# Transposes of x, B and the squares' sums moved from TensorE to VectorE squares of 32 placed by DMA

## The chip, the cores and the metric

The kernel runs on one core of one Trainium2 chip. The core has TensorE (PE in the profile, its weight loads PEld), VectorE (DVE), ScalarE (ACT), GpSimd (POOL), SyncE (SP), which here only issues transfers, and 16 DMA engines. The metric is the device time of one launch in microseconds; lower is better. The profile adds one execution under the hardware profiler.

## What is computed

A transformer-like layer in float32 on x of shape (8, 2048, 256): a layer norm with modulation from a condition, a state-space (Mamba-2) mixer, a gated residual, a second modulated layer norm, and a mixture of 8 experts whose weights are thresholded. All eight experts are computed for every token. The mixer, cut to what the change touches:

```python
zxbcdt = hidden_states @ W_in                    # z | x, B, C | dt
xBC = silu(causal_dwconv(xBC, conv_w, conv_b))   # 4 taps along the tokens
dt = softplus(dt + dt_bias)
# per chunk: scores C B^T times the decays, applied to x*dt; the state
# carries sum over tokens of B (x*dt) decay
y = ssd(x, dt, A, B, C) + x * D
y = y * silu(z)
y = y * rsqrt(mean(y * y, axis=-1) + EPS) * norm_w
return y @ W_out
```

## The kernel before, in words

The tokens are worked in 32 blocks of T = 512 (8 batch rows times 4), each in 4 chunks of 128. Channels lie on the 128 partitions and tokens along the free dimension after the projection: `xbc` holds x in four tiles of 128 channels (MI = 4), then B, then C.

The order of the work is a plan in Python. Each stage is a generator; `at` and `after` give due times, `until` waits for a step of the same plan, and a heap pops the stages by time (lines 192 to 209). The unit is meant as a microsecond, but only the order of emission comes out of it: the engines' queues and the framework's waits do the rest. Blocks start every PERIOD = 70 units; `STARTS` (L803) sets when each stage of a block is due, so several blocks are in work at once. The PSUM banks are handed out by the plan too: eight, with at most 3 for experts, 2 for projections, 2 for y, and 4 for everything else.

The stages of a block in order: `fetch` loads x; `first_norm` normalises and transposes it (L353, L355). `project_xbc` (L424) multiplies by the weights; `conv` adds the first tap on ACT (L379) and the three others on VectorE (L387). `steps_of_time` computes the decays and writes them to DRAM as `cs_d` (L505). `silu_xbc` (L442) and `project_z` (L460, silu in L447) follow. `spread` (L523) reads back the decays of a chunk over all partitions as `wide`. `within` handles a chunk: eight Relu steps on ACT (L538), four transposes of x (L548) and one of B (L549) on TensorE into two banks, the scores B^T C (L551), two exponentials (L552, L553); then on VectorE `xdt` = x times dt (L556) and `both` = (B, masked scores) out of PSUM (L560), on POOL `xdec` (L568), on VectorE `w` (L572), on POOL `cw` = C times decay (L575). L586 is the state's matmul, L589 and L600 carry the state on. For every two chunks `outputs` computes y (L618), adds D*x on VectorE, four instructions per chunk (L630), multiplies by silu(z) (L634), and sums squares over groups of channels into `sqs` (ACT L641, POOL L643, L644). `output` turns `sqs` on TensorE (L659), reduces it over the channels (L662), takes the inverse root, and multiplies by W_out (L672). Then come `residual`, `gate_weights`, and `experts` (matmuls L791, weighted sums on VectorE L748, last steps on POOL L756, L758, the store L761).

All transfers but one are issued by SP in order. An issue whose buffer is not free holds up those behind it.

Of the kernel before, what the change touches and what calls it, by code (L numbers as in the profile page):

```python
# [15 lines left out]
P = 128  # L16
# [4 lines left out]
EPS = 1e-5  # L21
GATE_MIN = 0.25
# [3 lines left out]
def kernel(  # L26
# [209 lines left out]

    def per_head(t):
        return t.unsqueeze(2).to_broadcast([P, NH, HEADDIM])
# [57 lines left out]
    def batch_gates(b):  # L296

        rows = new(pb, [P, KD, P], "rows", bufs=1)
# [77 lines left out]
    def conv(n, m, ps):  # L376

        acc = info[n]["xbc"][:, m, :]
        nc.scalar.activation(  # L379
# [53 lines left out]
    def silu_xbc(n):  # L433
# [3 lines left out]
        if order[n][1] > 0:  # L437
            yield from until(d, "fixed")
            nc.vector.tensor_add(xbc[:, :, :HALO], xbc[:, :, :HALO], info[n]["fix"])
            yield 0.4  # L440
        for m in range(0, MC, 2):
            nc.scalar.activation(xbc[:, m : m + 2, :], xbc[:, m : m + 2, :], AF.Silu)  # L442
            yield 2.0
        d["xbc_silu"] = True

# [73 lines left out]
    def spread(n, c):  # L519

        yield from until(info[n], "cs_d")
        wide = info[n]["wide", c] = new(chk, [P, NH, P], "wide")
# [3 lines left out]
        yield  # L526

    def within(n, c):
# [8 lines left out]
        for h in range(NH):  # L537
            nc.scalar.activation(  # L538
                w[:, h, :], wide[:, h, :], AF.Relu, bias=tok_major[:, 1, c, h : h + 1], scale=-1.0
            )  # L540
# [4 lines left out]
        yield from until(d, "xbc_silu")  # L545
        x_ps, b_ps = yield from take("m", 2)
        for m in range(MI):
            nc.tensor.transpose(x_ps[:, ts(m, P)], xbc[:, m, tok], ident)  # L548
        nc.tensor.transpose(b_ps[:, :P], bt, ident)  # L549

        nc.tensor.matmul(b_ps[:, P : 2 * P], bt, ct_, start=True, stop=True)  # L551
        nc.scalar.activation(wide, wide, AF.Exp)  # L552
        nc.scalar.activation(w, w, AF.Exp, scale=-1.0)  # L553
        yield 1.2
        xdt = new(chk, [P, DI], "xdt", bufs=3)
        nc.vector.tensor_tensor(  # L556
            by_head(xdt), by_head(x_ps[:, :DI]), per_head(tok_major[:, 0, c, :]), ALU.mult
        )
        both = new(chk, [P, 2, P], "both")
        nc.vector.tensor_mul(both, b_ps[:, : 2 * P].rearrange("p (n i) -> p n i", n=2), masks)  # L560
        bm, sm = both[:, 0, :], both[:, 1, :]
        give(x_ps)
        give(b_ps)
        last = s_of(n) == NSB - 1 and c == NC - 1
        yield 1.0
        if not last:
            xdec = new(chk, [P, DI], "xdec", bufs=1)
# [5 lines left out]
        yield 1.8  # L573
        cw = new(chk, [P, NH, P], "cw", bufs=3)
        nc.gpsimd.tensor_tensor(cw, wide, ct_[:, None, :].to_broadcast([P, NH, P]), ALU.mult)  # L575
        yield 2.0
# [4 lines left out]
        yield 3.5  # L581
        state = carry.get("state") if (s_of(n), c) != (0, 0) else None
        if not last:
# [3 lines left out]
            behind = new(blk, [P, DI], "state", bufs=4)  # L587
            if state is not None:
                nc.gpsimd.tensor_tensor(  # L589
                    by_head(behind), by_head(state), per_head(wide[:, :, P - 1]), ALU.mult  # L590
# [15 lines left out]
    def outputs(n, first):  # L606
# [17 lines left out]
        for j, y_ps in enumerate(pair):  # L624
# [4 lines left out]
            for m in range(MI):  # L629
                nc.vector.scalar_tensor_tensor(  # L630
                    y[:, m, :], xbc[:, m, tok], d_ch[:, m : m + 1], y[:, m, :],
                    ALU.mult, ALU.add,
                )
# [7 lines left out]
            nc.scalar.activation(sq, g[:, :, tok], AF.Square)  # L641
# [9 lines left out]
    def output(n):  # L651
# [4 lines left out]
        yield 5.0  # L656
        s_ps = yield from take("m")
        for c in range(NC):
            nc.tensor.transpose(s_ps[:, ts(c, P)], d["sqs"][:, c, :], ident)  # L659
        yield 1.2  # L660
        ms = new(sml, [P, NC], "ms")
        nc.vector.tensor_reduce(ms, s_ps.rearrange("p (c t) -> p c t", c=NC), AX.X, ALU.add)  # L662
        give(s_ps)
# [80 lines left out]
    def weighted(n, c, e, ps, res):  # L744
        wt = info[n]["wt"]
        per = 512 // DM
        for q in range(per):
            nc.vector.scalar_tensor_tensor(  # L748
# [16 lines left out]
    def experts(n):  # L765
# [34 lines left out]
    READ_TIME = 4.5  # L800
    WARM = 15
    PERIOD, XBC_STEP, Z_STEP, OUT_STEP = 70.0, 6.0, 3.5, 4.4
    STARTS = (  # L803
        (fetch, -20.0), (first_norm, -9.0), (project_xbc, 11.5), (project_z, 42.0),
        (silu_xbc, 47.5), (output, 128.0), (gate_weights, 156.0), (experts, 198.0),
# [6 lines left out]
    at(30.0, modulation(1))  # L812
    for n in range(len(order)):
        start = n * PERIOD
        for stage, delay in STARTS:
# [40 lines left out]
```

## Time and profile before

The profiled execution's numbers, with the median beside them:

| | |
|---|---|
| median of 3 runs | 2382.57 us (2381.75 to 2382.87) |
| the profiled execution's own time | 2381.93 us |
| its span, first to last instruction | 2380.1 us |
| mean granted TensorE clock | 0.993 of full speed |
| costliest group: expert matmuls, L791 | 2048 instructions, 963.3 us busy |
| costliest group of VectorE: weighted sums, L748 | 1024, 487.5 us busy |
| costliest group of ACT: Relu steps, L538 | 1024, 328.0 us busy |
| costliest group of POOL: `cw`, L575 | 128, 310.8 us busy |
| DMA packets | 64648 with 110.50 MB, 7096 of them under 512 B |

How to read the lines that follow: a group line names line, engine, operation, output <- inputs, their shapes (partitions x elements) and the count; after the first bar the busy time of the group and the mean length of one instruction in ns; after the second the idle time of its engine just before it and what ended that. The timeline gives start and length of each run of equal instructions. A line of stretches gives the stretch, its length, the busy us of the engines with the number of instructions, the granted clock, the mean busy share of the 16 DMA engines and GB/s. In the slices a digit is a tenth.

### The profile page before, as it was taken

The numbers are of one execution on the slowest core, as the hardware profiler recorded it, in microseconds if no ns is written. First come the engines' busy times: TensorE is split into PE (matmuls) and PEld (weight loads), VectorE is DVE, ScalarE is ACT, GpSimd is POOL, SyncE is SP. The second block draws the span as 40 slices with busy tenths as digits, with TensorE's granted clock in tenths as the row PEclk, the third lists the DMA queues.
The fourth block names the chain that finished last, engine by engine and source line by source line (L and its number), as shares of the span: only waits on it lengthen the run. The fifth ranks groups of instructions, "written<-read, shape, count | busy, mean of one in ns | idle before, by whom it ended". The sixth has DMA issues, their size and how long they took to land.

```text
span 2380.1 us, 33341 instructions
## 1 busy us (share of the span) xinstructions
PE 2317.9 (97%) x11632; PEld 1313.3 (55%) x11632; DVE 1816.6 (76%) x4188; ACT 1621.7 (68%) x2950; POOL 1128.4 (47%) x1245
## 2 busy tenths in 40 slices
PE   7899999999999999999999999999999999999998
PEld 4555555555555555555555555555555555555564
DVE  4777877778777787877877777878777787777775
ACT  6878766677666686666776667766776767667720
POOL 3554355453454454454544554544545444545442
PEclk8999999999999999999999999999999999999999
DMA  5111111110111111111110111111111101111100
GB/s 166 46 37 46 37 46 46 45 55 27 47 55 47 45 46 38 46 52 49 45 46 28 55 55 36 55 37 37 55 44 47 46 29 54 46 45 46 38 19 18
DMA packets 64648, 110.50 MB, mean 46 GB/s; under 512 B 7096, under 2 KB 47072, under 8 KB 64480
## 3 DMA queue, kind: packets, MB, share of 16 engines
q1 hardware_dynamic: 64464, 108.35, 13.8%
q8 instruction: 93, 1.52, 0.3%
q14 instruction: 75, 0.61, 0.1%
q10 hardware_dynamic: 16, 0.01, 0.0%
HBM read 89.47 MB, written 18.87 MB: 46 GB/s over the span
## 4 chain that ended last, share of the span: by engine, by line
PE 61%; ACT 10%; POOL 9%; DVE 6%; issue 1%; POOLq 0%; ACTq 0%; DVEq 0%
PE bank L791 26%; PE bank L672 8%; PE bank L424 7%; PE bank L460 6%; PE bank L618 4%; POOL cw L575 3%; PE bank L586 3%; ACT w L538 3%; DVE xbc L387 2%; PE bank L353 1%; PE bank L548 1%; ACT xbc L442 1%; POOL xdec L568 1%; POOL sq L643 1%; ACT wide L552 1%
## 5 line engine op out<-in xcount | busy, mean ns | idle before, releaser
L791 PE MATMUL bank<-we_sb,ht 128*128 128x512 f32 x2048 | 963.3, 595 | 3.3 <-DVE both L560 1.9
L748 DVE SCALAR_TENSOR_TENSOR res<-bank,wt,res 128x256 f32<-128x256 f32 x1024 | 487.5, 476 | 199.4 <-PE bank L791 112.7
L791 PEld LDWEIGHTS bank<-we_sb,ht 128*128 128x128 f32 x2048 | 374.0, 190 | 379.6 <-issue 352.1
L387 DVE SCALAR_TENSOR_TENSOR xbc<-bank,conv_w_sb,xbc 128x511 f32<-128x511 f32 (+2 forms) x576 | 425.8, 740 | 121.2 <-ACT halo L383 119.6
L575 POOL TENSOR_TENSOR cw<-wide,xbc 128x1024 f32<-128x1024 f32 x128 | 310.8, 2428 | 295.3 <-ACT wide L552 168.8
L538 ACT ACTIVATE w<-wide,tok_major 128x128 f32<-128x128 f32 x1024 | 328.0, 390 | 142.1 <-PE bank L618 100.8
L424 PE MATMUL bank<-ht,w_in_sb 128*128 128x512 f32 x768 | 369.1, 603 | 0.8 <-DVE xbc L387 0.8
L460 PE MATMUL bank<-ht,w_in_sb 128*128 128x512 f32 x512 | 244.4, 601 | 0.0
L672 PE MATMUL bank<-wo,zs 128*128 128x256 f32 x1024 | 243.5, 380 | 0.0
L589 POOL TENSOR_TENSOR state<-state,wide 128x512 f32<-128x512 f32 x112 | 120.8, 1079 | 232.7 <-DVE state L600 206.5
L424 PEld LDWEIGHTS bank<-ht,w_in_sb 128*128 128x128 f32 x768 | 140.4, 191 | 154.6 <-issue 139.5
L355 ACT ACTIVATE ht<-bank,mod_pp 128x512 f32<-128x512 f32 x128 | 97.4, 776 | 178.8 <-PE bank L353 178.7
L379 ACT ACTIVATE xbc<-bank,conv_b_sb,conv_w_sb 128x512 f32<-128x512 f32 x192 | 147.3, 767 | 104.3 <-PE bank L424 104.3
L672 PEld LDWEIGHTS bank<-wo,zs 128*128 128x128 f32 x1024 | 189.6, 191 | 48.9 <-issue 23.4
L568 POOL TENSOR_TENSOR xdec<-xdt,tok_major 128x512 f32<-128x512 f32 x120 | 142.0, 1183 | 141.9 <-DVE xdt L556 141.4
L756 POOL TENSOR_TENSOR res<-res,gates 128x256 f32<-128x256 f32 x128 | 134.9, 1054 | 151.8 <-DVE res L748 144.4
L343 ACT ACTIVATE xn<-xt,shift,rstd 128x256 f32<-128x256 f32 x256 | 137.5, 591 | 82.0 <-DVE shift L339 74.9
L572 DVE TENSOR_TENSOR w<-w,both 128x1024 f32<-128x1024 f32 x128 | 191.6, 1497 | 1.4
L630 DVE SCALAR_TENSOR_TENSOR bank<-xbc,d_ch,bank 128x128 f32<-128x128 f32 x512 | 175.6, 350 | 20.2 <-PE bank L618 10.9
L586 PE MATMUL bank<-xdec,both 128*128 128x512 f32 x240 | 128.6, 618 | 17.6 <-POOL xdec L568 12.8
L460 PEld LDWEIGHTS bank<-ht,w_in_sb 128*128 128x128 f32 x512 | 91.2, 191 | 96.5 <-issue 91.2
L643 POOL TENSOR_TENSOR sq<-sq 128x256 f32<-128x256 f32 x128 | 98.0, 766 | 91.3 <-ACT sq L641 73.4
(130 smaller groups left out, 3333.2 us busy)
## 6 DMA issues: line engine op xcount, KB each, us to landing
wide<-cs_d SPq DMA_DIRECT2D x128, 512.0 KB
out_dram<-xt SPq DMA_DIRECT2D x32, 512.0 KB
xt<-_attn_hidden_states_dram SPq DMA_DIRECT2D x31, 512.0 KB
cs_d<-cs SPq DMA_DIRECT2D x32, 64.0 KB
we_sb<-in_L_ffn_expert_w_dram SPq DMA_DIRECT2D x8, 256.0 KB
ht<-in_L_wmod_dram SPq DMA_DIRECT2D x2, 512.0 KB
w_in_sb<-in_L_attn_W_in_dram SPq DMA_DIRECT2D x1, 776.0 KB
xt<-_attn_hidden_states_dram SPq DMA_DIRECT2D x4, 128.0 KB
```

The lines of the kernel that those rows point to most:

```text
L387: nc.vector.scalar_tensor_tensor(acc[:, ahead:], ps[:, : T - ahead], conv_w_sb[:, m, k : k + 1], acc[:, ahead:], ALU.mult, ALU.add,)
L424: nc.tensor.matmul(ps, w_in_sb[:, k, DI + m * P : DI + (m + 1) * P], ht[:, k, :], start=(k == 0), stop=(k == KD - 1),)
L460: nc.tensor.matmul(ps, w_in_sb[:, k, ts(m, P)], ht[:, k, :], start=(k == 0), stop=(k == KD - 1),)
L538: nc.scalar.activation(w[:, h, :], wide[:, h, :], AF.Relu, bias=tok_major[:, 1, c, h : h + 1], scale=-1.0)
L568: nc.gpsimd.tensor_tensor(by_head(xdec), by_head(xdt), per_head(tok_major[:, 2, c, :]), ALU.mult)
L572: nc.vector.tensor_tensor(w, w, sm[:, None, :].to_broadcast([P, NH, P]), ALU.mult)
L575: nc.gpsimd.tensor_tensor(cw, wide, ct_[:, None, :].to_broadcast([P, NH, P]), ALU.mult)
L586: nc.tensor.matmul(st_ps[:, :DI], bm, xdec, start=True, stop=True)
L630: nc.vector.scalar_tensor_tensor(y[:, m, :], xbc[:, m, tok], d_ch[:, m : m + 1], y[:, m, :], ALU.mult, ALU.add,)
L672: nc.tensor.matmul(o_ps[:, :DM], d["zs"][:, m, ts(c, P)], wo[:, m, :], start=(m == 0), stop=(m == MI - 1),)
L748: nc.vector.scalar_tensor_tensor(res, ps[:, ts(q, DM)], wt[:, c, e + q : e + q + 1], res, ALU.mult, ALU.add)
L791: nc.tensor.matmul(ps, ht[:, k, ts(c, P)], we_sb[:, k, e : e + per, :].rearrange("p e o -> p (e o)"), start=(k == 0), stop=(k == KD - 1),)
```

## The change

Three transposes leave TensorE. In all blocks but the first, each of the four x tiles and the B tile is transposed by VectorE in squares of 32x32 (one instruction for 128 channels x 512 tokens), and four writes per tile put the squares' rows (runs of 32 numbers) at their turned place in a DRAM buffer `turned` (512 tokens x 640 channels). One load per chunk brings back 128 tokens x 640 channels as `xtok`, and x*dt is formed in place in it. In all blocks but the last, the squares' sums are transposed and reduced by VectorE in the same way: partial sums per group of 32 channels go to DRAM and come back by four loads, and a small reduce adds them. The first block keeps the transposes of x and B on TensorE, the last one those of the sums.

ACT multiplies x by D in place after the transpose has read it, so that one addition on VectorE replaces four instructions per chunk; the first block keeps the four. `cw` is now formed in the buffer of `wide` (four buffers instead of two), after the last column of `wide` was saved as `whole`, and earlier in the chunk. `xdec` gets a second buffer, `state` goes from four buffers to three. `rows` shares the buffer of `sign`. The mask for B is gone, since B is no longer multiplied by ones. `follow` adds an ordering, without a wait, behind the last marked instruction of the same engine. Several due times move: the table of starts is in the diff.

```diff
+    def follow(engine, second):
+        if engine in pace:
+            tc.add_manual_dep(
+                second.ins, pace[engine].ins.name,
+                mybir.DependencyInfo(mybir.DependencyClass.NoSync, mybir.DependencyReason.DATA),
+                reason="in the order of emission",
+            )
...
+        if n > 0:
+            d["turned"] = new(dram, [T, (MB + 1) * P], "turned")
         for m in range(0, MC, 2):
             nc.scalar.activation(xbc[:, m : m + 2, :], xbc[:, m : m + 2, :], AF.Silu)
-            yield 2.0
+            for q in range(m, min(m + 2, MB + 1) if n > 0 else m):
+                after(3.0 + 2.0 * (q - m), turn_tile(n, q))
+            yield 4.0 if n > 0 else 2.0
         d["xbc_silu"] = True
+
+    def turn_tile(n, m):
+
+        d = info[n]
+        squares = new(blk, [P, T], "squares", bufs=3)
+        nc.vector.transpose(squares, d["xbc"][:, m, :])
+        yield 2.5
+        places = d["turned"].rearrange("(b i) r -> i b r", i=SQ)
+        for a in range(P // SQ):
+            nc.sync.dma_start(
+                out=places[:, :, m * P + a * SQ :][:, :, :SQ],
+                in_=squares[ts(a, SQ), :].rearrange("i (b j) -> i b j", j=SQ),
+            )
+        d["turned", m] = True
+        yield 3.0
+        if m < MI:
+
+            x = d["xbc"][:, m, :]
+            follow("act", nc.scalar.activation(x, x, AF.Copy, scale=d_ch[:, m : m + 1]))
...
-        wide = info[n]["wide", c] = new(chk, [P, NH, P], "wide")
+        wide = info[n]["wide", c] = new(chk, [P, NH, P], "wide", bufs=4)
...
+    def turn(n, c):
+
+        d = info[n]
+        if n == 0:
+            return
+        yield from until(d, *(("turned", m) for m in range(MB + 1)))
+        xt = new(chk, [P, DI + P], "xtok", bufs=3)
+        nc.sync.dma_start(out=xt, in_=d["turned"][ts(c, P)])
+        yield TURN_TIME
+        d["xtok", c] = xt
...
-        yield from until(d, "xbc_silu")
-        x_ps, b_ps = yield from take("m", 2)
-        for m in range(MI):
-            nc.tensor.transpose(x_ps[:, ts(m, P)], xbc[:, m, tok], ident)
-        nc.tensor.transpose(b_ps[:, :P], bt, ident)
-
-        nc.tensor.matmul(b_ps[:, P : 2 * P], bt, ct_, start=True, stop=True)
         nc.scalar.activation(wide, wide, AF.Exp)
         nc.scalar.activation(w, w, AF.Exp, scale=-1.0)
+        yield from until(d, "xbc_silu")
+        yield 1.5
+
+        whole, cw = new(chk, [P, NH], "whole", bufs=3), wide
+        nc.gpsimd.tensor_copy(whole, wide[:, :, P - 1])
+        nc.gpsimd.tensor_tensor(cw, wide, ct_[:, None, :].to_broadcast([P, NH, P]), ALU.mult)
+        yield 1.5
+        yield from until(d, "xbc_silu" if n == 0 else ("xtok", c))
...
+        else:
+            s_ps = yield from take("m")
+
+        nc.tensor.matmul(s_ps[:, :P], bt, ct_, start=True, stop=True)
         yield 1.2
-        xdt = new(chk, [P, DI], "xdt", bufs=3)
-        nc.vector.tensor_tensor(
-            by_head(xdt), by_head(x_ps[:, :DI]), per_head(tok_major[:, 0, c, :]), ALU.mult
-        )
+        xdt, bm = d["xtok", c][:, :DI], d["xtok", c][:, DI:]
+        second = nc.vector.tensor_tensor(
+            by_head(xdt), by_head(x_ps[:, :DI] if n == 0 else xdt), per_head(tok_major[:, 0, c, :]),
+            ALU.mult,
+        )
...
-            xdec = new(chk, [P, DI], "xdec", bufs=1)
+            xdec = new(chk, [P, DI], "xdec")
...
+            if n > 0:
+                nc.vector.tensor_tensor(y, y, xbc[:, :MI, tok], ALU.add)
...
+            squares = new(blk, [P, T], "squares", bufs=3)
+            follow("dve", nc.vector.transpose(squares, d["sqs"].rearrange("p c t -> p (c t)")))
+            part = new(sml, [P, NC * NS], "part")
+            nc.vector.tensor_reduce(
+                part, squares.rearrange("p (q j) -> p q j", j=SQ), AX.X, ALU.add
+            )
+            yield 2.5
+            part_d = new(dram, [NS, SQ, NC, NS], "part_d")
+            nc.sync.dma_start(out=part_d.rearrange("a i c b -> (a i) (c b)"), in_=part)
+            yield 3.5
+            parts = new(sml, [P, NC, NS], "parts")
...
+                for q in range(NS):
+                    nc.sync.dma_start(
+                        out=parts[ts(q, SQ)].unsqueeze(3),
+                        in_=part_d[:, :, :, q : q + 1].rearrange("a i c b -> i c a b"),
+                    )
+            yield TURN_TIME
+            follow("dve", nc.vector.tensor_reduce(ms, parts, AX.X, ALU.add))
...
+    TURN_TIME = 12.0
...
-        (fetch, -20.0), (first_norm, -9.0), (project_xbc, 11.5), (project_z, 42.0),
-        (silu_xbc, 47.5), (output, 128.0), (gate_weights, 156.0), (experts, 198.0),
+        (fetch, -20.0), (first_norm, -9.0), (project_xbc, 11.5), (project_z, 48.0),
+        (silu_xbc, 47.5), (output, 144.0), (gate_weights, 190.0), (experts, 232.0),
...
+    first = {
+        project_z: 42.0, silu_xbc: 40.0, output: 112.0, gate_weights: 134.0, experts: 170.0,
+    }
...
-            at(start + c * PERIOD / NC + 44.0, spread(n, c))
-            at(start + c * PERIOD / NC + 54.0, within(n, c))
+            step = start + c * PERIOD / NC
+            at(step + (36.0 if n == 0 else 44.0), spread(n, c))
+            at(step + 59.0, turn(n, c))
+            at(step + (44.0 if n == 0 else 65.0), within(n, c))
```

## The prediction

> **What bounds the kernel now.** I read the page's busy lines first, then the wait list and the groups of TensorE by shape, then the timeline of one block, and last the transfers in narrow stretches. From the page, the busy time by engine and the slices:
>
> ```profile
> PE 2317.9 (97%) x11632; PEld 1313.3 (55%) x11632; DVE 1816.6 (76%) x4188; ACT 1621.7 (68%) x2950; POOL 1128.4 (47%) x1245
> PE   7899999999999999999999999999999999999998
> DMA  5111111110111111111110111111111101111100
> ```
>
> TensorE is in use almost everywhere, the next engine for 76%. A sum over three stretches (us from the start: length, then the busy us of PE, PEld, DVE, ACT, POOL, the granted clock, the DMA share, GB/s) shows where it is idle:
>
> ```profile
> 0.00:148.00 148.00, 119.50 (x646) 70.00 (x647) 102.31 (x224) 116.61 (x213) 65.54 (x87) 0.93 0.30 93
> 148.00:2310.00 2162.00, 2135.22 (x10796) 1212.03 (x10795) 1677.37 (x3876) 1499.58 (x2727) 1048.27 (x1139) 1.00 0.13 44
> 2310.00:2380.00 70.00, 63.22 (x193) 31.26 (x191) 36.89 (x89) 5.46 (x11) 14.57 (x21) 0.98 0.07 23
> ```
>
> Until the first expert matmul (148 us) 28.5 us are idle, in the last 70 us 6.8, and in the 2162 us between only 26.8. Each block takes about 72 us there (an output store at 1241.7, the next at 1314.1) and TensorE's work sets that. What it waits for most, by the wait list of PE (total us, times, longest), is small:
>
> ```profile
> PE bank L586 <- POOL xdec L568: 12.8, 22, 1.5
> PE bank L659 <- POOL sqs L644: 6.0, 4, 3.4
> ```
>
> So work taken from TensorE in the middle stretch shortens the kernel by as much, as long as nothing new makes TensorE wait.
>
> **What is taken from TensorE.** The three groups that go (busy us, mean ns, idle before), and one chunk of them in the timeline (start, us, instruction):
>
> ```profile
> L548 PE MATMUL bank<-ident,xbc 128*128 128x128 f32 x512 | 77.9, 274 | 2.7 <-ACT xbc L442 2.7
> L549 PE MATMUL bank<-ident,xbc 128*128 128x128 f32 x128 | 35.4, 277 | 3.7 <-ACT xbc L442 2.9 <-DVE xdt L556 0.8
> L659 PE MATMUL bank<-ident,sqs 128*128 128x128 f32 x128 | 20.4, 276 | 6.0 <-POOL sqs L644 6.0
> ...
> 1200.88 0.60 PE L548 MATMUL bank<-ident,xbc 128*128 128x128 f32 x4
> 1201.31 0.27 PE L549 MATMUL bank<-ident,xbc 128*128 128x128 f32 x1
> 1201.42 0.39 PE L551 MATMUL bank<-xbc 128*128 128x128 f32 x2
> 1201.64 1.88 PE L791 MATMUL bank<-we_sb,ht 128*128 128x512 f32 x4
> ```
>
> Busy time overstates them: a record of 0.27 us overlaps the next. From start to start, five transposes take 1201.42 - 1200.88 = 0.54 us, so 0.108 each, and the expert matmul follows without a gap. The change removes 31 blocks x (4 chunks x 5 + 4) = 744 of them: 744 x 0.108 = 80 us. I take this and not the 129 us that the busy column gives (133.7 x 31/32).
>
> **What is put on the other engines, per block.** VectorE gains six transposes of 128x512 and a small reduce. No row shows a transpose; the nearest form is an operation over 128x512, 0.68 us (L634, 686 ns). Bounds: 0.34, half of that, and 1.5, the price of 128x1024 (L572). It gains 6 x 0.68 + 0.18 = 4.3 us; the reduce over 512 remains. It loses, in each of four chunks, three of four D*x steps (4 x 0.350 - 0.686 = 0.71) and half of the product with the masks (0.414 - 0.275 = 0.14): 3.4 us. Net +0.9 us, 27 us in all: 1817 to about 1844, 80% of 2300. At 1.5 us a transpose it would be 87%: hidden behind TensorE either way. ACT gains four in-place products of 128x512 at 0.62 (L641), 2.5 us a block or 77 us in all, to 1699 (74%). Its 288 table loads of 1.28 us can shift with the order; one more per block is 40 us, still hidden. POOL gains a copy of 128x8, about 0.2 us x 128 = 26 us (the 128x4 and 128x18 rows are 0.2), to 1154 (50%). `cw` in place costs nothing: the same instruction, earlier. What covers all three is TensorE's load of about 69.5 us per block; without that cover VectorE would set some 58 us.
>
> **The transfers.** SP gets, per block, 20 writes of 32 partitions x 16 pieces of 128 B, four loads of 320 KB, one write of the partial sums and four loads of 512 single numbers: 29 issues of 0.33 to 0.38 us, about 10 us of a queue that mostly waits. Their price on the DMA engines is the weak point. The trace has these stretches (same columns as above; a write of 128 pieces of 512 B, an output store of 512 pieces of 1 KB, and a stretch in which, by the issue times, the 1536 pieces of 4 and 16 B of the convolution's constants fell):
>
> ```profile
> 1202.20:1202.60 0.40, 0.40 (x3) 0.16 (x2) 0.40 (x2) 0.40 (x1) 0.00 (x0) 1.00 0.58 163
> 1242.50:1245.00 2.50, 2.50 (x12) 1.68 (x11) 2.36 (x6) 2.47 (x3) 2.50 (x2) 1.00 0.64 216
> 7.80:8.80 1.00, 1.00 (x6) 1.00 (x6) 0.00 (x0) 0.00 (x0) 0.00 (x0) 1.00 1.39 170
> ```
>
> Share x time x 16 engines / pieces: 29 ns for 512 B, 50 ns for 1 KB. In the third, 22 engine-us less 8.3 for its 170 KB at the second row's rate leave about 9 ns per tiny piece. A line through the two stores gives 13 ns for 128 B; I take 16, between bounds of 9 and 58. The upper bound is where the trace and the skill part: the Trainium skill, "DMA: Bandwidth & Descriptors", section Specifications, says that pieces under 512 B are read, modified and written, so I double the 512 B row. At 16 ns one tile (2048 pieces) drains in 2.0 us, and a block adds about 164 + 64 + 27 engine-us (pieces, loads, sums), 16 us of each engine: a share of 0.37 instead of 0.14.
>
> **The new wait.** VectorE's product `xdt` now waits for a load, where it waited for TensorE. Behind it on VectorE stand convolution steps and the experts' sums (L748), and TensorE waits for those once its three "ex" banks are full, 4.4 plan units apart. By the plan's due times, in a block's own time, the last transpose (B) is emitted at 58.9, and the first chunk's `xdt` at 74.6, 15.7 units later (a unit is about 1 us here). The chain: 0.7 transpose, 1.4 four issues, 0.8 to the first byte (a write issued at 1201.37 moved bytes from 1202.2), 2.0 to drain, 0.6 to land (SP issued the dependent load at 1203.1), 0.9 issue and start, 1.6 for 320 KB: 8.0. It has 7.7 to spare. Later chunks have 12 units for a load alone; the sums have 12 for theirs. ACT's in-place D*x waits for VectorE's transpose, emitted 5.5 units before it, with convolution steps behind it; at VectorE's load of 80% I count nothing, and the bound of the last term below covers it. TensorE's state matmul (L586) follows the score matmul by 12.1 units instead of 10.1, with POOL's `cw` out of the way and a second `xdec`, so most of its 12.8 us of waits should go.
>
> **The rule that speaks against it.** The same page, section Rules for kernel authors, gives a plain DMA with a rearranged access pattern as 19 times slower than the hardware transpose. By the rule: 512 KB took 2.1 us at a share of 0.74 (stretch 1203.9 to 1206.0), so 256 KB 0.78 us, x 19 = 15 us a tile, 74 us a block; with 15 us of other traffic the DMA engines would set 89 us, 31 x 89 + 100 = about 2860. By the rows it is 2 us a tile, because here VectorE turns the squares and the transfer keeps runs of 32 numbers. I go by the rows.
>
> **Longer pipeline.** From the second block on, experts start at 232 instead of 198, the first block's at 170: a gap of 62 plan units with no expert matmul. By the fill (148 us for 228 units) that is 40 us, in which TensorE idles perhaps 4 us (9% between 70 and 210 us) and runs slower for some; the first stretch gets 28 units shorter and gives some back. I take +5, bounds 0 and +34 (34 units more of length with nothing beside them).
>
> **The sum.** Against the profiled execution, 2381.9 us (span 2380.1 and 1.8 around it; the median of the runs is 0.6 higher): -80 transposes, -8 waits for `xdec`, +5 fill, +5 for new waits of VectorE and SP (0 to 35, about a microsecond a block at most) = 2304.
>
> **Rivals.**
> 1. The transposes were worth their busy time, or lost gaps go with them: 2381.9 - 129 = 2253. For: the busy column. Against: the start times. Reach 2252 to 2285. 5%.
> 2. Part is given back: the fill costs its full 34 and VectorE waits a little on each first chunk: 2304 + 29 + 10 = 2343 (2325 to 2377). For: ACT at 91% and TensorE's idle in the 70 us after 70. 12%.
> 3. Slower: the 128 B pieces at 58 ns. A tile takes 7.4 us but tiles come 2 units apart, so from 52.8 the five end at 90 and the load at 93, 18 after VectorE reaches `xdt`. VectorE has about 12 us idle a block; some 6.5 us a block stay: 31 x 6.5 = +200, 2504. It outweighs the gain of 2.6 us a block from about 52 ns a piece on. At the rule's 117 ns it is the 2860 above. Against: 29 ns for pieces four times as large, 9 ns for tiny ones. 19%.
> 4. Nothing measurable: between 47 and 52 ns the two cancel: 2382. 4%.
>
> **How the numbers follow.** Likeliest (60%): TensorE stays the bound, 2304, own range 2285 to 2325. A measurement tells about 0.2% (4.8 us) from no change. Faster is the likeliest with rivals 1 and 2, 77%; same 4%; slower 19%. The range 2252 to 2387 leaves out rival 3.
>
> **What would show it.** Right: the transposes of L548, L549 and L659 left only in 16, 4 and 4 instances, block distance near 69.5 us, TensorE still about 97%, DVE near 1840, DMA share near 0.37. Wrong: a large wait of VectorE's `xdt` product for the load of `xtok`, with expert matmuls waiting for VectorE; a DMA share over 0.6; a row for the transpose over 1.5 us; TensorE idle growing from 62 us by more than 20.

## The result and the profile after

The changed kernel takes 2424.4 us (median of 4 runs, 2422.7 to 2425.1) against 2382.7 for the kernel before beside it: a ratio of 1.0174, 95% interval 1.0157 to 1.0192. It is slower by 1.7%; the forecast was 2304, faster by 3.3%, with a range up to 2387. Its profiled execution has a span of 2423.3 us and a mean granted clock of 0.983 (before: 2380.1 and 0.993). In the ratios here and below, executions more than 1.5% above the fastest of their kernel are left out, which concerns three of the 15 of dxdve_slack alone.

From the page after, the busy times, the slices of TensorE and of the DMA engines:

```profile
PE 2277.2 (94%) x10888; PEld 1241.4 (51%) x10888; DVE 1867.4 (77%) x4037; ACT 1588.9 (66%) x3002; POOL 1156.2 (48%) x1373
PE   6779999999999999999999999999999999999998
DMA  5232324233233243234233242233323333243310
```

The 744 matmuls are gone (11632 - 10888), yet TensorE is idle for 146 us where it was idle for 62. The first two of the three stretches as before (up to the first expert matmul, and the middle):

```profile
0.00:155.00 155.00, 116.68 (x552) 65.45 (x553) 98.53 (x209) 101.77 (x195) 63.67 (x91) 0.89 0.37 106
155.00:2353.00 2198.00, 2097.29 (x10152) 1146.21 (x10150) 1733.38 (x3746) 1480.55 (x2795) 1078.16 (x1261) 0.99 0.33 79
```

In the middle the idle time is 2198 - 2097 = 101 us; it was 27. The wait list of PE between 470 and 2230 us, 24 blocks, says for whom (total us, times, longest):

```profile
PE bank L547 <- ACT sp_e L543: 21.7, 18, 1.2
PE bank L645 <- POOL xdec L630: 16.6, 18, 0.9
PE bank L437 <- ACT ht L368: 12.7, 30, 0.7
PE bank L865 <- ACT wtt L828: 11.5, 19, 0.6
PE bank L794 <- ACT head L792: 9.9, 24, 0.4
```

None is long, but they come in most blocks: with 2.5 us for `halo`, 74.9 us, or 3.1 a block. Before, `xdec` was the only one that came often (11.9 us, 20 times). Four of the five are short steps of ACT that TensorE needs at once: the decays' exponential (`sp_e`), the normed and modulated tokens (`ht`), the experts' weights (`wtt`), the gate's logits (`head`).

To place the loss I take the first expert matmul of each block from the timeline. Block 0 to 4 is the start, block 4 to 28 gives the time of a block:

| kernel | start (first expert of block 4) | a block | rest after block 28's | span |
|---|---|---|---|---|
| before | 444.5 | 72.41 | 197.8 | 2380.1 |
| after | 473.8 | 73.12 | 194.6 | 2423.3 |

The span grew by 43.2: 29.3 in the start, 24 x 0.71 = 17.0 in the middle, -3.1 at the end. Against the forecast the block is the larger miss: it was to fall to about 69.5.

A block's time splits into three parts: the idle time of TensorE, the time lost to a halved clock (half of each stretch in which the granted clock is 0.50), and the rest, in which TensorE works at full clock. From the profiled executions, blocks 4 to 28, us a block, with four of the runs described below:

| kernel | idle | halved clock | rest | a block |
|---|---|---|---|---|
| before | 0.76 | 0.07 | 71.58 | 72.41 |
| after | 3.10 | 0.50 | 69.52 | 73.12 |
| strip | 1.02 | 0.07 | 68.86 | 69.95 |
| stripsched | 2.21 | 1.00 | 69.20 | 72.40 |
| ss_g156 | 0.36 | 0.00 | 68.71 | 69.07 |
| g230 | 1.54 | 0.14 | 69.46 | 71.14 |

So TensorE's own work did fall, by 2.06 us a block, and 2.77 us of waits and halved clock outweigh that.

What the forecast feared did not happen. The product in `xtok`, the transposes of x and ACT's product with D (group lines: busy us, mean ns, idle before), and SP's waits for the pieces to land (total us, times, longest):

```profile
L614 DVE TENSOR_TENSOR xtok<-xtok,tok_major 128x512 f32<-128x512 f32 x124 | 126.1, 1017 | 0.0
L467 DVE STREAM_TRANSPOSE squares<-xbc 128x512 f32<-128x512 f32 x155 | 106.2, 697 | 7.6 <-ACT xbc L457 6.0 <-DMA turned<-squares 1.4
L480 ACT ACTIVATE xbc<-xbc,d_ch 128x512 f32<-128x512 f32 x124 | 85.2, 713 | 3.1 <-DVE squares L467 1.6
SPq L571 <- DMA turned<-squares: 8.7, 19, 0.6
```

VectorE never stood idle before L614: no load was late. The last 2560-byte piece of each load landed at least 1.87 us before the product began.

### The profile page after: what moved, and what is told of

It is laid out like the page before. It is cut to its first block, busy times and chain, and to the rows that moved or that the text cites. A ratio compares the mean times of both kernels' runs of the same rounds, so it can differ in the third digit from the quotient of the medians.

```text
span 2423.3 us, 33631 instructions
## 1 busy us (share of the span) xinstructions
PE 2277.2 (94%) x10888; PEld 1241.4 (51%) x10888; DVE 1867.4 (77%) x4037; ACT 1588.9 (66%) x3002; POOL 1156.2 (48%) x1373
## 4 chain that ended last, share of the span: by engine, by line
PE 44%; ACT 20%; DVE 17%; POOL 14%; issue 4%; DMA 1%; SPq 0%; POOLq 0%; DVEq 0%; ACTq 0%
PE bank L878 15%; PE bank L437 9%; PE bank L759 7%; ACT w L585 6%; PE bank L677 6%; POOL wide L599 5%; ACT wide L592 3%; PE bank L645 3%; DVE xbc L400 3%; PE bank L496 3%; DVE res L835 2%; DVE squares L467 2%; POOL xdec L630 2%; ACT ht L368 2%; DVE xtok L614 2%
## 5 line engine op out<-in xcount | busy, mean ns | idle before, releaser
L835 DVE SCALAR_TENSOR_TENSOR res<-bank,wt,res 128x256 f32<-128x256 f32 x1024 | 485.4, 474 | 111.7 <-PE bank L878 95.2
L400 DVE SCALAR_TENSOR_TENSOR xbc<-bank,conv_w_sb,xbc 128x509 f32<-128x509 f32 (+2 forms) x576 | 424.9, 740 | 78.4 <-ACT halo L396 75.3
L599 POOL TENSOR_TENSOR wide<-wide,xbc 128x1024 f32<-128x1024 f32 x128 | 303.0, 2367 | 11.1 <-ACT xbc L457 1.0
L598 POOL COPY whole<-wide 128x8 f32<-128x8 f32 x128 | 24.7, 193 | 565.3 <-ACT wide L592 565.3
L703 ACT ACTIVATE sq<-zs 128x512 f32<-128x512 f32 x128 | 80.3, 627 | 246.8 <-DVE zs L696 112.6
L630 POOL TENSOR_TENSOR xdec<-xtok,tok_major 128x512 f32<-128x512 f32 x120 | 127.6, 1065 | 215.5 <-DVE xtok L614 207.4
L843 POOL TENSOR_TENSOR res<-res,gates 128x256 f32<-128x256 f32 x128 | 102.2, 799 | 220.9 <-DVE res L835 213.9
L634 DVE TENSOR_TENSOR w<-w,sm 128x1024 f32<-128x1024 f32 x128 | 189.6, 1481 | 5.9 <-ACT w L593 2.5
L645 PE MATMUL bank<-xdec,xtok 128*128 128x512 f32 x240 | 136.0, 652 | 24.4 <-POOL xdec L630 24.3
L705 POOL TENSOR_TENSOR sq<-sq 128x256 f32<-128x256 f32 x128 | 114.5, 895 | 78.4 <-ACT sq L703 76.2
L677 PEld LDWEIGHTS bank<-w,xtok 128*64 128x64 f32 x2048 | 114.7, 138 | 56.9 <-issue 42.8
```

The lines of the kernel that those rows point to most:

```text
L400: nc.vector.scalar_tensor_tensor(acc[:, ahead:], ps[:, : T - ahead], conv_w_sb[:, m, k : k + 1], acc[:, ahead:], ALU.mult, ALU.add,)
L630: nc.gpsimd.tensor_tensor(by_head(xdec), by_head(xdt), per_head(tok_major[:, 2, c, :]), ALU.mult)
L634: nc.vector.tensor_tensor(w, w, sm[:, None, :].to_broadcast([P, NH, P]), ALU.mult)
L645: nc.tensor.matmul(st_ps[:, :DI], bm, xdec, start=True, stop=True)
L677: nc.tensor.matmul(y_ps[ts(q, HEADDIM), ts(m, P)], lhs[:, ts(h, HEADDIM)], rhs[:, h, :], start=(i == 0 and m == 0), stop=(i == len(parts) ...
L835: pace["dve"] = nc.vector.scalar_tensor_tensor(res, ps[:, ts(q, DM)], wt[:, c, e + q : e + q + 1], res, ALU.mult, ALU.add)
```

## The experiments

The table gives all runs by what they measured: the median, the ratio to the kernel before on the same chip with its interval, and from the profiled execution the start and the time of a block as above. The profiled execution of dxdve_slack is the fastest of its 15, that of stripsched the slowest of its 20 (2388.75).

| run | median us | ratio | start | block |
|---|---|---|---|---|
| strip | 2316.8 | 0.9725 (0.9710 to 0.9739) | 445.8 | 69.95 |
| sched | 2395.8 | 1.0055 (1.0040 to 1.0070) | 471.6 | 72.38 |
| stripsched | 2383.7 | 1.0007 (1.0000 to 1.0013) | 466.7 | 72.40 |
| ss_w54 | 2365.5 | 0.9926 (0.9911 to 0.9940) | 464.1 | 72.08 |
| ss_g156 | 2285.3 | 0.9592 (0.9578 to 0.9607) | 434.6 | 69.07 |
| strip_dx | 2314.3 | 0.9719 (0.9705 to 0.9734) | 440.1 | 70.09 |
| nofollow | 2474.8 | 1.0389 (1.0373 to 1.0404) | 477.8 | 75.07 |
| nopin_act | 2442.4 | 1.0250 (1.0235 to 1.0265) | 474.6 | 73.80 |
| dx_nopin | 2420.0 | 1.0152 (1.0137 to 1.0167) | 467.1 | 73.17 |
| cwlate | 2427.0 | 1.0181 (1.0164 to 1.0198) | 473.3 | 73.26 |
| dxdve | 2367.4 | 0.9935 (0.9918 to 0.9951) | 455.4 | 71.67 |
| dxdve_w61 | 2358.6 | 0.9897 (0.9880 to 0.9913) | 464.6 | 70.96 |
| g230 | 2390.9 | 1.0034 (1.0020 to 1.0047) | 518.8 | 71.14 |
| sums_pe | 2524.5 | 1.0593 (1.0577 to 1.0609) | 477.8 | 77.46 |
| sums_pe_g156 | 2452.7 | 1.0293 (1.0276 to 1.0310) | 457.4 | 74.44 |
| after_slack | 2447.0 | 1.0279 (1.0247 to 1.0312) | 485.4 | 73.98 |
| dxdve_slack | 2401.0 | 1.0067 (1.0045 to 1.0089) | 474.0 | 71.81 |
| before_slack | 2399.3 | 1.0069 (1.0054 to 1.0084) | 438.5 | 73.49 |

**Is the removal worth what was forecast?** Two theories: the transposes cost TensorE 0.108 us each and taking them away shortens the kernel by that; or TensorE's load hid chains over the other engines, which now show.

strip:

```diff
-        for m in range(MI):
-            nc.tensor.transpose(x_ps[:, ts(m, P)], xbc[:, m, tok], ident)
-        nc.tensor.transpose(b_ps[:, :P], bt, ident)
+        if n == 0:
+            for m in range(MI):
+                nc.tensor.transpose(x_ps[:, ts(m, P)], xbc[:, m, tok], ident)
+            nc.tensor.transpose(b_ps[:, :P], bt, ident)
...
+            nc.vector.tensor_reduce(ms, d["sqs"], AX.X, ALU.add)
```

> The kernel before, with the 744 transposes left out and nothing put in their place: from the second block on, x*dt is formed from x as it lies (not turned), the state's matmul takes B as it lies, and the squares' sums are reduced as they lie (except in the last block), so the result differs from the reference. If the transposes really cost TensorE 0.108 us each and TensorE is the bound, as the prediction has it: 2383 - 80 = 2303, with about 70 us a block. If taking work from TensorE only uncovers chains over the other engines that were hidden behind it: above 2340, with TensorE idle where it was busy.

Measured 2316.8, -66 us; the block fell from 72.41 to 69.95, so by 2.46 where the forecast's 80 / 31 is 2.58. In a block the removal is worth nearly what was said; in all it is 66 of the 80 us. The changed kernel, at 2424, loses 107 us elsewhere.

**The due times alone.** sched: the kernel before with the changed table of starts, `first` and the offsets 44, 65 and 36, 44.

> The kernel before, with nothing but the due times of the changed kernel. If the loss is the longer pipeline at the start (the distance between the experts of the first and second block grew from 76.9 to 101.2 us, and the fifth block's experts begin 29 us later): +25 to +30, 2410, with 72.4 us a block kept in the middle. If the due times also order the queues worse in every block: above 2430. If the fill is lost through the transfers and not through the due times: within 5 of 2383.

Measured 2395.8: the block is unchanged, the start grows by 27.1 us (444.5 to 471.6), and 13 come back at the end. So the due times alone can make 27 of the changed kernel's 29 us in the start, and the forecast's +5 for them was too small. The parts do not simply add up, though: dxdve below has the same due times and starts only 10.9 us later than the kernel before.

stripsched: the same due times in the stripped kernel.

> The stripped kernel (transposes left out, nothing put in their place, result not the reference's) with the due times of the changed one. If the due times let latency-critical steps meet ACT's exponentials and so make TensorE wait in every block: near 73 us a block, 2410. If the due times cost only the start, as they do in the kernel before: 70 us a block, 2317 + 13 = 2330; what is left to 2424 then belongs to the added instructions, transfers and pins.

Measured 2383.7 with 72.40 us a block: the whole gain of the stripped kernel is gone. Due times that cost nothing in the middle while TensorE carried the transposes cost 2.45 us a block without them. This is the second theory, but only for this order of the work. Of the 2.45 us, 1.2 are idle time and 0.9 the halved clock.

**Which stage's due time.** ss_w54 puts the chunk stage back, ss_g156 the output, gates and experts:

```diff
-            at(step + (44.0 if n == 0 else 65.0), within(n, c))
+            at(step + (44.0 if n == 0 else 54.0), within(n, c))
```

```diff
-        (silu_xbc, 47.5), (output, 144.0), (gate_weights, 190.0), (experts, 232.0),
+        (silu_xbc, 47.5), (output, 128.0), (gate_weights, 156.0), (experts, 198.0),
```

> The stripped kernel with the changed due times (2384), but the chunk stage within back at 54 from the second block on; output, gates and experts stay late, work is left out as in the stripped kernel. If the chunk stage's place among ACT's other work is what makes TensorE wait: 70 us a block, 2330. If the late gates are (TensorE waited there for ht and head): 72.4 us a block, 2384.

> The stripped kernel with the changed due times, but output, gates and experts at their old due times (they then wait in the plan for what they need); within stays at 65, work left out as in the stripped kernel. If the late gates cause the waits for ht and head: 70 us a block, 2325. If the chunk stage does: 72.4 us a block, 2375.

Measured 2365.5 (72.08 a block) and 2285.3 (69.07 a block). It is mainly the late output, gates and experts; the chunk stage's place is worth 0.32 us a block. The wait lists of PE, first stripsched (470 to 2200 us), then ss_g156 (470 to 2090 us):

```profile
PE bank L708 <- ACT ht L355: 34.4, 17, 3.6
PE bank L716 <- ACT head L714: 16.7, 14, 1.5
```

```profile
PE bank L424 <- ACT ht L355: 8.2, 15, 1.5
```

With the gates due at 190, that is 50 of the period's 70 units, the second norm of one block meets silu(z), a chunk's Relu steps and the first norm of a later block in ACT's queue. The timeline of ACT in stripsched (start, length, instruction, idle before) shows one such meeting, and that of PE what waits for it (L353 are the transposes that `ht` is made from, L708 the gate's matmuls that read it):

```profile
1381.26 0.40 ACT L538 ACTIVATE w<-wide,tok_major 128x128 f32<-128x128 f32 x1 [2.98 <-DVE res L757]
1381.68 1.28 ACT L553 ACT_TABLE_LOAD   x1
1382.97 1.06 ACT L553 ACTIVATE wide<-wide 128x1024 f32<-128x1024 f32 x1
1383.94 0.76 ACT L355 ACTIVATE ht<-bank,mod_pp 128x512 f32<-128x512 f32 x1
```

```profile
1378.34 0.66 PE L353 MATMUL bank<-ident,xn 128*128 128x128 f32 x4
...
1384.75 0.59 PE L708 MATMUL bank<-ht,gate_w_sb 128*32 128x128 f32 x8 [2.41 <-ACT ht L355]
```

TensorE has given the second half of `ht` at 1379.0. ACT stands 2.98 us in front of a Relu step; behind that step wait a table load and an exponential, and only then comes `ht`, 4.9 us after it could have. TensorE waits 2.41 us of that. `head` is late in the same way in another block:

```profile
1459.56 0.63 ACT L646 ACTIVATE sq<-zs 128x512 f32<-128x512 f32 x1 [1.54 <-POOL sqs L649]
1460.09 0.25 ACT L714 COPY head<-bank 128x128 f32<-128x128 f32 x1
...
1460.39 0.33 PE L716 MATMUL bank<-ident,head 128*128 128x128 f32 x1 [1.42 <-ACT head L714]
```

TensorE had given it at 1456.6; ACT had four steps of another norm before it, and one that waited for POOL. Each of these engines worked through its queue in order here, so a step that waits holds up a short one behind it, and TensorE with it.

**Does that hold in the changed kernel?** There the gates can't simply be earlier, since by the plan's due times the sums' detour over DRAM keeps output at about 170. g230 moves them and the experts on instead, the gates to 20 of 70 units (with six x buffers instead of five and two for the squares instead of three):

```diff
-        (silu_xbc, 47.5), (output, 144.0), (gate_weights, 190.0), (experts, 232.0),
+        (silu_xbc, 47.5), (output, 144.0), (gate_weights, 230.0), (experts, 272.0),
```

> The changed kernel with gates due at 230 and experts at 272 instead of 190 and 232, so that the gates fall at 20 of the period's 70 units and not at 50 (six buffers for x, two for the squares, since blocks live longer). If the place of the gates is what costs: 70 to 71 us a block, less 2 to 3 us times 27, plus some 20 for the longer start: 2355 to 2385. If not: 73 us a block and the longer start, 2440.

Measured 2390.9: the block falls by 1.98 us to 71.14, with every part of the change in place. The start grew by 45 us, more than the 20 I had expected, of which the end gives back 31. Idle time and halved clock make 1.92 of the 1.98 us. From 520 to 2220 us PE's waits for `sp_e` are gone, those for `ht` down to 0.7 us in all; the longest left:

```profile
PE bank L645 <- POOL xdec L630: 17.1, 18, 1.8
PE bank L865 <- ACT wtt L828: 9.0, 13, 2.1
```

But the waits of the changed kernel are not all like those of the stripped one. Its two longest, for `sp_e` and `xdec`, in one of the 18 blocks of the list that have them (start, length, instruction, idle before):

```profile
469.85 1.04 ACT L593 ACTIVATE w<-w 128x1024 f32<-128x1024 f32 x1
470.91 1.28 ACT L530 ACT_TABLE_LOAD   x1
472.20 0.31 ACT L530 ACTIVATE sp_l<-sp_u 128x128 f32<-128x128 f32 x1
472.55 0.29 DVE L532 SCALAR_TENSOR_TENSOR sp_u<-sp_u,sp_e 128x128 f32<-128x128 f32 x1 [1.53 <-ACT sp_l L530]
475.44 1.28 ACT L543 ACT_TABLE_LOAD   x1 [2.04 <-DVE cs L538]
...
477.19 0.33 PE L547 MATMUL bank<-ident,sp_e 128*128 128x128 f32 x1 [1.21 <-ACT sp_e L543]
478.21 1.04 POOL L630 TENSOR_TENSOR xdec<-xtok,tok_major 128x512 f32<-128x512 f32 x1 [5.58 <-DVE xtok L614]
479.30 1.87 PE L645 MATMUL bank<-xdec,xtok 128*128 128x512 f32 x2 [0.92 <-POOL xdec L630]
```

Nothing stands in front of `sp_e` on ACT: ACT was idle for 2.04 us, waiting for VectorE's `cs`. VectorE had waited 1.53 us for the decays' logarithm (`sp_l`), and that stood behind a chunk's exponential (L593) and its own table load on ACT. Likewise POOL was idle for 5.58 us in front of `xdec`, waiting for VectorE's `xtok`, which came behind a convolution step and a weighted sum in VectorE's queue. So these two, half of the 74.9 us, are chains that go through two engines' queues; that the gates' place lengthens them is shown by g230, how it does is not.

sums_pe and sums_pe_g156 turn the squares' sums on TensorE in every block, the second with the old due times of ss_g156:

```diff
-        if n == len(order) - 1:
+        if True:
             yield 5.0
```

> The changed kernel with the squares' sums turned by TensorE in every block (124 transposes more, 13 us of TensorE). If the detour over VectorE, DRAM and SP for the sums costs more than it saves: below 2424, by up to 30. If not: 2424 + 13 = 2437, or 2424 where TensorE waits anyway.

> The changed kernel with the squares' sums turned by TensorE in every block and output, gates and experts at their old due times (the same kernel with the late due times took 2524). If the place of the gates in the period is what costs: some 70 us a block, 13 us more TensorE work than the stripped kernel's 2285, 2305 to 2330, faster than the kernel before. If the changed order of the rest costs by itself: 72 us a block or more, above 2370.

Measured 2524.5 and 2452.7. The first is outside all that I had expected; the second is what was named for a changed order that costs by itself. The early due times are worth 72 us here too, but the kernel stays at 74.44 us a block, so the gates' place is not the whole of it. In sums_pe_g156, from 490 to 2180 us: ACT stands 176 us in front of `xn` for VectorE's `shift` (18 times, up to 12.7 us), and TensorE 36 us in front of `head`. Why this order is so much worse than the changed one I have not settled.

**D*x on ACT.** dxdve leaves it on VectorE:

```diff
-            if n > 0:
-                nc.vector.tensor_tensor(y, y, xbc[:, :MI, tok], ALU.add)
-            else:
-                for m in range(MI):
+            for m in range(MI):
...
-            x = d["xbc"][:, m, :]
-            follow("act", nc.scalar.activation(x, x, AF.Copy, scale=d_ch[:, m : m + 1]))
```

> The changed kernel with D*x as before (four instructions of VectorE a chunk, no product in place on ACT). If ACT's added 2.9 us a block make TensorE wait for sp_e, ht, wtt and head: a block falls by 1 to 3 us, 2340 to 2395. If ACT's load is not it, VectorE's 2.9 us more a block can only hurt: 2424 to 2450.

Measured 2367.4: 57 us faster than the changed kernel and faster than the kernel before, although VectorE does more (1952 us busy). Of the 57, 18 lie in the start, 35 in the 24 blocks and 5 at the end. TensorE's waits for `sp_e` did not fall (26.0 us from 470 to 2200 us, against 21.7 in the changed kernel), those for `xdec` are gone from the list. dx_nopin leaves D*x on ACT without its pin; strip_dx puts it on ACT in the stripped kernel with the old due times:

> The changed kernel with D*x on ACT but without its pin (the Relu steps keep theirs). If D*x on ACT costs by where the pin puts it: near 2367, as with D*x on VectorE. If it costs by ACT's 2.9 us a block: 2424. If free placement is worse, as it was without any pin on ACT: near 2442.

> The stripped kernel (old due times, work left out as there) with D*x formed in place by ACT and one addition on VectorE. If ACT's 2.9 us a block cost by themselves: 1.5 us a block, 2360. If they only cost together with the moved stages: 2317 within 8.

Measured 2420.0 and 2314.3. It is not the pin, and D*x on ACT costs 0.14 us a block by itself, which is nothing in the total. It costs 57 us only in this order of the work; why is not shown. The detour over VectorE and DRAM itself costs nothing that shows: dxdve has all of it and is 16 us faster than stripsched, the stripped kernel with the same due times.

**The pins and POOL's order.** nofollow makes `follow` do nothing, nopin_act keeps only VectorE's pins, cwlate moves POOL's `cw` back behind `w`:

```diff
-        if engine in pace:
+        if engine == "dve" and engine in pace:
```

> The changed kernel without its ordering pins (the marked instructions are free to move in the framework's order). If the pins hold ACT and VectorE in an order that makes TensorE wait (ACT stood 362 us in front of a projection's result, 104 before): the block falls from 73.1 to about 70 us, 2340 in all. If the pins protect from a transfer that is late: slower than 2424, with waits of VectorE for the load of xtok. If the pins do nothing here: 2424.

> The changed kernel with the pins of VectorE alone; ACT's Relu steps and D*x are free to move. If ACT's pins (362 us of ACT standing in front of a projection) make TensorE wait: faster than 2424, 71 us a block, 2370. If it was the lack of ACT's pins that made the kernel without any pin slow: near 2475. If VectorE's pins were the ones that protect: 2424.

> The changed kernel with the product of wide and C (and the copy ahead of it) back behind the product of w, where it stood before. POOL stood 565 us in front of that copy, waiting for ACT's exponential, with xdec, rstd and the squares' sums behind it. If that is what makes TensorE wait (24 us for xdec): xdec's waits nearly gone, 1 to 2 us less a block, 2370 to 2395. If POOL's order does not matter: 2424 within 5.

Measured 2474.8, 2442.4 and 2427.0. ACT stood 362 us in front of a projection's result and POOL 565 us in front of `whole`, the two longest waits of these engines, and neither is a cause: without ACT's pins the first fell to a third (from 288 us to 104, from 470 us on), yet the kernel is slower, and `cw`'s place does not matter.

**More time for the late steps.** If TensorE only reaches those steps too early, later due times should help. The edit, in three kernels:

```diff
-        yield 7.0
+        yield 11.0
         t_ps = yield from take("m")
...
-        yield 1.0
+        yield 3.0
         keep["ht", half] = ht
...
-        yield 3.5
+        yield 5.5
         nc.tensor.transpose(lg_ps[:, P : 2 * P], head, ident)
...
+        yield 2.5
+        d["wtt"] = wtt
```

The state's matmul goes 2 later, first_norm is due 2 earlier and the experts 8 later.

> The changed kernel with later due times for the steps in front of which TensorE waited: the decays' transposes 4 units later, both normed halves 2, the gate head's transpose 2, the experts' weights 2.5, the state's matmul 2. If the loss is that TensorE reaches these before ACT or POOL has finished, because their distance in TensorE's queue was meant for a busier TensorE: the waits of 3.1 us a block and the clock's halvings go, 70 to 71 us a block, about 2350. If the waits only move to other instructions: 2424 within 15.

> The same later due times with D*x left on VectorE. If the waits for sp_e (1.4 us a block with the DVE scan) and ht are what is left there: from 2367 to about 2325, 70 us a block, faster than the kernel before by 2%. If they only move: 2367 within 15.

> The kernel before with the same later due times, as a control. It waits 0.8 us a block, so there is little to win: 2383 within 10, if later due times do nothing by themselves; faster by 15 or more if they are good for any order.

Measured 2447.0, 2401.0 (its runs lay between 2379.9 and 2426.3) and 2399.3: all slower. The waits for `sp_e` are gone in both changed kernels, but those for `xdec` grew, from 16.6 to 42 us in the one and from nothing in the list to 41 in the other, and even the kernel before got slower by 1.1 us a block. In after_slack the idle time of a block stays at 3.1 us while the halved clock takes 1.9 instead of 0.5. So the simple form of the theory, too little time at each step, falls: the wait comes back elsewhere. I put this down to the other engines' orders, which a later due time moves too; no run shows that apart.

**A version that beats both.** dxdve_w61: D*x on VectorE, and the chunk stage due at 61 instead of 65.

> The changed kernel with D*x on VectorE (2367) and the chunk stage due at 61 instead of 65, so that its exponentials come ahead of the decays' logarithm and not into it. If that meeting makes TensorE wait for sp_e (1.4 us a block): 70.3 us a block, 2335. If it only moves the waits: 2367 within 15.

Measured 2358.6, 1.0% faster than the kernel before. PE's waits for `sp_e` fell from 26.0 to 4.2 us over 24 blocks, as meant, which fits the reading above. But 40.2 us of waits for `xdec` came up, so all waits of the list fell only from 54.4 to 44.4 us and the block by 0.7.

## Why the prediction was wrong

**What TensorE loses: right, and nearly in size.** 744 transposes less; 16, 4 and 4 are left, as forecast. Their price from start to start, 80 us, and not the busy column's 129, is what the stripped kernel shows (66 in all, 2.46 us a block, which over 31 blocks is 76). In the changed kernel TensorE's own work fell by 2.06 us a block instead of 2.58; where the other 0.5 went no run shows. Rival 1 is out.

**What the other engines gain: right in size.** A transpose 0.697 us (0.68 forecast), the one addition in y 0.693 (0.686), `whole` 0.193 (0.2), D*x on ACT 0.713 (0.62). Busy sums: VectorE 1867 (1844; `xdt` takes 1.02 us on average instead of 0.68, which the forecast missed; the last section says when), POOL 1156 (1154), ACT 1589 (1699; its table loads fell from 290 to 218). None of these sums bounds the kernel, as said.

**The transfers: right.** The DMA share in the middle is 0.33 (0.37 forecast). The rise of 0.20 over 73.1 us is 234 engine-us a block; less the forecast's 64 and 27 for loads and sums, 143 for 10240 pieces: an estimate of 14 ns each, near the 16 that was taken and far from the 58 of the upper bound. The forecast's estimate by the rule of 19 times was 74 us a block; nothing of that kind shows. Rivals 3 and 4 are out, and the new wait of VectorE for `xtok` is 0.0.

**The new waits: wrong, and this is the step that failed.** The sum had "+5 for new waits of VectorE and SP (0 to 35, about a microsecond a block at most)", and "most of its 12.8 us of waits should go" for `xdec`. The waits were TensorE's own, on ACT and POOL, 3.1 us a block, and `xdec`'s grew to 24.3. In the terms of the table by parts, the forecast comes to 69.7 us a block: 71.58 less 2.58 of work, 0.66 idle, 0.07 halved clock. Measured are 3.4 more: 2.4 idle, 0.4 halved clock, 0.5 work that did not go. Of the prediction's signs of being wrong only the last came, TensorE's idle time growing by more than 20 us; it grew by 84.

I had looked at each added wait alone and asked whether its own chain had time to spare. I had not asked what the moved stages meet in the queues they are moved to. Shown: the late output, gates and experts cost it in the stripped kernel (72.40 against 69.07 us a block), and the place of gates and experts in the changed one (73.12 against 71.14, with two buffer counts changed). The mechanism, short steps behind long or waiting ones in the queues of ACT and VectorE, is read off the timeline of single blocks. One run aimed at one such meeting: the chunk's exponentials in front of the decays' logarithm, and with these moved the waits for `sp_e` went from 26.0 to 4.2 us. For the others no run isolates it from the reordering that any new due time brings.

**D*x on ACT: its price "I count nothing" was wrong by 57 us**, but only in the changed order. The forecast asked whether ACT's product would wait for VectorE's transpose (1.6 us in all, so it hardly did), not what it would move on ACT.

**The start: mis-sized.** +5 with a bound of 34; it measured +29; the due times alone make 27 in the kernel before, and dxdve, with the same due times, has 11. The forecast took TensorE's idle share of another stretch; the distance between the first and second block's experts went from 76.9 to 101.2 us. The end gave back 3.

**The clock: not in the sum.** Mean granted clock 0.983 instead of 0.993: by that (1 - 0.983) x 2423 = 41 us of the span are lost to it instead of 17, 10 of the difference in the start and 10 in the 24 blocks. Rival 2 had the start's full price but no cause for a loss in every block, and ended below the kernel before.

Open: why D*x on ACT and the sums on TensorE cost as much as they do in this order, how the gates' place reaches the waits for `sp_e`, and where 0.5 us of TensorE's work a block stayed.

## What to carry to other kernels

When work is taken from the busiest engine, and at the same time stages are moved to make room for a detour, cost the two apart: the first is a sum of slots, the second is a new order in every in-order queue, and a bound at 97% holds only for the old one. For each stage that moves, list the short steps that the busiest engine needs at once and look at what stands in front of them at the new place in the period. A kernel with the removal alone, one with the new due times alone, and one with both tell which of the two went wrong. The third is needed: here the first two gave -66 and +13 us, and both together +1, where their sum would be -53.

## What the runs showed of the hardware

**Two short waits close together can be followed by half TensorE's clock.** The timeline of PE after, and four stretches (their columns are those of the stretches above; the granted clock is the third number from the end):

```profile
402.45 0.33 PE L547 MATMUL bank<-ident,sp_e 128*128 128x128 f32 x1 [1.20 <-ACT sp_e L543]
...
404.56 2.07 PE L645 MATMUL bank<-xdec,xtok 128*128 128x512 f32 x2 [0.92 <-POOL xdec L630]
```

```profile
401.05:404.46 3.41, 1.38 (x5) 0.36 (x3) 3.41 (x6) 2.29 (x4) 1.00 (x1) 1.00 0.41 118
404.46:407.87 3.41, 3.31 (x4) 1.51 (x5) 2.31 (x6) 0.00 (x0) 3.41 (x6) 0.50 0.13 46
694.59:698.00 3.41, 1.69 (x6) 0.51 (x4) 3.41 (x6) 2.60 (x4) 0.69 (x1) 1.00 0.38 118
698.00:701.42 3.42, 3.01 (x7) 1.44 (x8) 3.38 (x8) 0.00 (x0) 3.42 (x6) 1.00 0.04 14
```

Two waits of 1.20 and 0.92 us within 3.4 us, and the clock is at 0.50 for the next 3.4 us, in which the two matmuls of L645 take 2.07 us; they take 1.12 at 698.41, where the clock stayed. The same pair of waits stands in 20 blocks from 402 us on, and only nine of them, seven in blocks 4 to 28, are followed by a halved clock. The nine halved stretches lie whole multiples of 3.413 us apart (479.55 - 404.46 = 22 x 3.413). Cut at these points, the stretch ahead of each of the nine has 1.77 to 2.09 us of idle TensorE, and no stretch of the eleven other pairs has more than 1.72: there the waits fell on both sides of a cut, or nearly so. The last two lines show the closest of them. So what counted was the idle share of such a stretch, about half, and not the single wait. In other runs the edge is less sharp: 1.69 us was followed by a halved clock (sums_pe), 1.97 was not (strip_dx). The Trainium skill, "TensorE: Matmul & The Clock Gate", section Why this matters for your kernels, advises against idle gaps above about 3 us; here gaps of about 1 us, two together, did it.

**A product of two SBUF operands on VectorE was slower beside POOL's work.** Of the 124 products L614 after, the 69 with no POOL instruction beside them took 0.65 to 0.68 us, the six that ran beside POOL's `cw` product alone (L599, 2.4 us) 2.68 to 2.71. In the kernel before, where the same product reads x from PSUM (L556), 77 of 128 ran beside a POOL instruction, and none took over 0.70.
